# Weight stacks of a convolution made on GpSimd alone and spread over more steps, and a table request moved to the end of a layer

## The chip, the cores and the metric

The kernel runs on one core of a Trainium2 chip. The core has five engines, each with a queue of its own that it works off in order: TensorE (PE, whose weight loads are shown as PEld), VectorE (DVE), ScalarE (ACT), GpSimd (POOL) and SyncE (SP, which here only starts transfers). The metric is the device time of one execution in microseconds; the figure for a kernel is the median of its runs.

## The reference, cut to what matters

A network of four layers, each an attention-like part and a feed-forward part with a residual sum and a layer norm behind each, is applied to `x` of shape (2, 1024, 1024) in float32:

```python
x = _layernorm(x + _L0_attn_ref(x, ...))   # 8 heads of 16, softmax over 1024 keys
x = _layernorm(x + _L0_ffn_ref(x, ...))    # permuted columns, per head up, gelu, down, permuted back
x = _layernorm(x + _L1_attn_ref(x, ...))   # a convolution over 3 positions gives q, k, v; attention in blocks of 128
x = _layernorm(x + _L1_ffn_ref(x, ...))    # product with the signs of the weights, routed scales
x = _layernorm(x + _L2_attn_ref(x, ...))   # selective scan
...                                        # L2_ffn, L3_attn, L3_ffn
```

What the change touches is the preparation of the weights of the convolution in layer 1 and the logarithm and exponential that the layer norms use.

The convolution is

```python
x = lax.conv_general_dilated(inputs, conv_w, window_strides=(1,), padding='SAME', ...) + conv_b
```

with `conv_w` of shape (3, 1024, 768). The kernel computes four neighbouring outputs at a time from six combinations of the inputs, each multiplied with its own combination of the three weight matrices g0, g1, g2. Two of the six are g0 and g2 themselves; the other four are g0 + g1 + g2, g0 - g1 + g2, g0 + 2 g1 + 4 g2 and g0 - 2 g1 + 4 g2 (constant factors are applied to the products later).

## The kernel before, in words

The kernel works through the two batches (b = 0, 1) one after the other, and through all layers for each. All 1024 tokens of a batch stay on chip, as `x` (tokens on the partitions, in eight tiles of 128) and as `xT` (channels on the partitions). `th` names a half of 512 tokens.

The order of the work is written out by hand inside blocks (`with self.tc.manual_schedule()`): within such a block each engine takes its instructions in the order of the program. There is one such block in `l0`, and several in `l1_attn`, one in `l1_ffn`.

**Layer 0 (`l0`).** The block goes through these steps:

- `qkv`: projections to queries, keys and values (L318), eight matmuls for each half, evicted by DVE (L327) or ACT (L325). Queries and keys are spread to their places by eight transfers each on SP's queue (L332); values are transposed on PE (L338) and copied by ACT (L341).
- `maxima(0)`: 16 steps, in each of which PE makes scores (L362) and DVE takes their maxima (L372). The remaining projections (`side`) are laid between these steps.
- `attend(0, turns)`: 16 steps; scores (L397), exponentials on ACT (L405), weighted sums (L415). `turns` adds a step of `maxima(1)` to each.
- `attend(1, e, ...)`: 16 steps of the same for the second half; `e` adds the output projection (L473, L482), the norm of the first four token tiles (statistics L169, L170; `ln_roots`, `ln_scale`, L192), the transposes to `xT` (L136; L103 on DVE, L105 on ACT), the transfers of `xT` to `xd` on SP (`store(tt)` of the layer, L487), and the gathers of permuted rows (`gather(0)`, L497: indirect transfers on GpSimd's queue).
- `blocks(0, e, ...)` and `blocks(1, e)`: per head pair the up product (L515), gelu on ACT (L523), the down product (L533), and an indirect transfer out to `yd` on GpSimd's queue (L546).

**The stacks.** In batch 0 alone, `stacks()` computes the four weight combinations for 24 blocks of 128 x 256 numbers. It is a generator: each `next(made)` does one step. For a block, `load(n)` starts three transfers on SP (L274), `make(n)` does six additions on GpSimd (L280, L282, L284, L285, L286, L288) and three multiplications on ACT (L281, L283, L287), and `store(n)` starts four transfers on SP to `cvd` in DRAM (L292). Three sets of buffers are used in turn: two weight tiles and `third`. Steps are taken from step 6 of `maxima(0)` on, one in every step, through the 16 steps of `attend(0)`. Layer 1's convolution reads `cvd` when it starts.

**The norms' roots.** `ln_roots` calls `rsqrt`: a logarithm (L183) and an exponential (L184) on ACT, then a correction on DVE (L186 to L189). ACT has to hold a table with the function it computes. `table()` asks for the one with both:

```python
def table(self):
    if self.other:
        self.nc.scalar.preload_act_table_set("natural_log_exp_and_others")
    self.other = False
```

`self.other` is set where gelu or silu is used. A load that was asked for shows in the profile as ACT_TABLE_LOAD at L199; one that was put in because a function's table was not there shows at the line of that function (L183, L184, L523, L1284). `l1_attn` calls `table()` at L820, in the middle of its first hand-ordered block, ahead of `root(4)` to `root(7)`, which are the roots of the second half's tiles. No other ACT instruction stands ahead of that call in that block.

The functions as they stand:

Of the kernel before, what the change touches and what calls it, by code (L numbers as in the profile page):

```python
# [8 lines left out]
F = mybir.dt.float32  # L9
# [3 lines left out]
ALU = mybir.AluOpType  # L13
# [4 lines left out]
P = 128  # L18
# [9 lines left out]
class Net:  # L28
# [191 lines left out]
    def l0(self, b):  # L220
        nc, i = self.nc, self.i
# [15 lines left out]
        with self.tc.tile_pool(name=self.nm("l0a"), bufs=1) as lp, self.tc.tile_pool(name=self.nm("l0b"), bufs=2) as tp:  # L237
# [24 lines left out]

            if b == 0:
                self.cvd = self.dp.tile([6, 4, P, D], F, name=self.nm("cvd"))
                third = lp.tile([P, 4, 256], F, name=self.nm("third"))

            def stacks():

                sets = [self.w().rearrange("p (a c) -> p a c", a=4) for _ in range(2)] + [third]
                add = nc.gpsimd.tensor_tensor  # L270

                def load(n):
                    for j in (0, 2, 1):
                        nc.sync.dma_start(  # L274
                            sets[n % 3][:, j, :], i["l1_conv"][n // 4, j][:, n % 4 * 256 : n % 4 * 256 + 256]
                        )

                def make(n):
                    g0, g1, g2, t = [sets[n % 3][:, j, :] for j in range(4)]
                    add(t, g0, g2, ALU.add)  # L280
                    nc.scalar.mul(g2, g2, 4.0)  # L281
                    add(t, t, g1, ALU.add)  # L282
                    nc.scalar.mul(g1, g1, 2.0)  # L283
                    add(g0, g0, g2, ALU.add)  # L284
                    add(g2, t, g1, ALU.subtract)  # L285
                    add(g0, g0, g1, ALU.add)  # L286
                    nc.scalar.mul(g1, g1, 2.0)  # L287
                    add(g1, g0, g1, ALU.subtract)  # L288

                def store(n):  # L290
                    for e, j in enumerate((3, 2, 0, 1)):
                        nc.sync.dma_start(  # L292
                            self.cvd[n // 4, e][:, n % 4 * 256 : n % 4 * 256 + 256], sets[n % 3][:, j, :]
                        )

                load(0)
                load(1)
                yield
                for n in range(24):
                    make(n)  # L300
                    if n:
                        store(n - 1)
                    if n + 2 < 24:
                        load(n + 2)
                    yield
                store(23)
                yield

            nmax = [piece("nmax").rearrange("p (a c) -> p a c", a=4) for _ in range(2)]
            for t in nmax:  # L310
# [274 lines left out]
            def at(extra, n, f):  # L585
                extra.setdefault(n, []).append(f)

            got = {}
            with self.tc.manual_schedule():
                self.table()  # L590
                for s in (1, 0):
                    for _ in qkv(s, 0, False):
                        pass
                for tt in range(4, NT):
                    self.to_xT(tt)
                for tt in range(4, NT):
                    self.add_row(row, tt)
                side = [
                    f for s, th in ((1, 1), (0, 1), (2, 0), (2, 1)) for f in [qkv(s, th, True)]
                    for _ in range(5 if s == 2 else 4)  # L600
                ]
                m0 = maxima(0)
                for n in range(16):
                    next(m0)
                    if b == 0 and n == 6:
                        made = stacks()
                    if b == 0 and n >= 6:
                        next(made)
                    for f in side[: 2 if n < 2 else 1]:
                        next(f)  # L610
                        del side[0]
                for f in side:
                    next(f)
                m = maxima(1)
                turns = {n: [lambda: next(m)] for n in range(16)}
                turns[0].insert(0, lambda: next(m0))
                if b == 0:
                    for n in range(16):
                        turns[n].append(lambda: next(made))
                done0 = attend(0, turns)  # L620
                e = line(0, project, (0, 1, 3, 4, 5, 6, 7, 8, 9))
                e[0].insert(0, lambda: next(m))
                for n in range(4):
                    at(e, 6 + n, lambda n=n: store(n))
                at(e, 9, lambda: gather(0))
                ahead = {n: [lambda tt=tt: turn_o(tt)] for tt, n in enumerate((0, 1, 3, 4))}
                done = attend(1, e, ahead, lambda: done0(1))
                e = line(1, project, (0, 0, 1, 1, 2, 3, 3, 4, 4))
                for n, tt in ((3, 4), (3, 5), (4, 6), (4, 7)):
                    at(e, n, lambda tt=tt: store(tt))  # L630
                for n in (5, 6):
                    at(e, n, lambda: gather(1, 2))
                ahead = {n: [lambda t=t: turn_o(t), lambda t=t: turn_o(t + 1)] for n, t in ((0, 4), (1, 6))}
                blocks(0, e, ahead, lambda: done(1))
                ys = back(0)
                e = line(0, lambda tt: self.add_y(tt, ys), (3, 3, 4, 4, 5, 6, 6, 7, 7))
                for n in (0, 1):
                    at(e, n, lambda: gather(1, 2))
                blocks(1, e)
        return yd[1]  # L640


# [3 lines left out]
    def l1_attn(self, b, yd, op):  # L646
        nc, i = self.nc, self.i
        row = self.row("l1_projb")
        with self.tc.tile_pool(name=self.nm("l1a"), bufs=1) as lp, self.tc.tile_pool(name=self.nm("l1s"), bufs=2) as spool:
# [138 lines left out]
            c = [conv(0, co) for co in range(6)]  # L788
# [8 lines left out]
            with self.tc.manual_schedule():  # L797
                if b == 0:
                    nc.vector.tensor_scalar(cb6, cb, -6.0, None, ALU.mult)
                    nc.vector.tensor_scalar(bq8, bq, 0.125, None, ALU.mult)  # L800
                for co, j in (
                    [(co, j) for j in (1, 2, 3, 0, 4) for co in (0, 1)] + [(2, 1), (2, 2), (2, 3), (0, 5), (1, 5)]
                    + [(2, 4), (2, 0), (2, 5)] + [(co, j) for co in (3, 4, 5) for j in ORDER]
                ):
                    c[co]["load"](j)
                pump()
                ys = [t for q in range(4) for t in (vh[:, q, :HALF], vh[:, q, HALF:])]
                for k, t in enumerate(ys):
                    nc.sync.dma_start(t, yd[k * P : (k + 1) * P, :])
                for k0, k1 in ((0, 2), (2, 4), (4, KD)):  # L810
                    sums(0, one, k0, k1)
                    c[0]["calls"](1, k0, k1)
                product(1, 1)
                product(0, 2)
                product(1, 2)
                sums(0, two)
                product(0, 3)
                product(1, 3)
                sums(0, [c_] + three)
                self.table()  # L820
                self.add_y(4, ys)
                root(4)
                product(0, 0)
                product(1, 0)
                self.add_y(5, ys)
                product(0, 4)
                c[0]["both"]()
                product(1, 4)
                c[1]["both"]()
                self.to_xT(4)  # L830
                sums(0, [e_] + five)
                root(5)
                for j in (1, 2, 3):
                    product(2, j)
                self.add_y(6, ys)
                for co in (0, 1):
                    product(co, 5)
                    c[co]["last"]()
                self.to_xT(5)
                root(6)  # L840
                product(2, 4)
                self.add_y(7, ys)
                product(2, 0)
                c[2]["both"]()
                product(2, 5)
                c[2]["last"]()
                self.to_xT(6)
                root(7)
                later = {
                    (3, 4): [lambda: self.to_xT(7)], (3, 5): [lambda: sums(1, [c_] + one)], (4, 2): [lambda: sums(1, two)],  # L850
                    (4, 4): [lambda: sums(1, [e_])], (5, 2): [lambda: sums(1, three + five)],
                }
                for co in (3, 4, 5):
                    for j in ORDER:
                        product(co, j)
                        if j == 0:
                            c[co]["both"]()
                        for f in later.get((co, j), []):
                            f()
                    c[co]["last"]()  # L860
# [171 lines left out]
            with self.tc.manual_schedule():  # L1032
# [42 lines left out]
                for name in ("l1_ics", "l1_ocs"):  # L1075
                    src, out = self.w(i[name], 32)[:32, :], self.w()[:32, :].bitcast(R)
                    part = self.l1p["l1_part"]
# [1331 lines left out]
```

## Time and profile before

| What | Value |
|---|---|
| Three runs | 4877.68, 4885.57 (median), 4892.11 us |
| The profiled execution | 4882.62 us, of which 4880.8 us are the span of its instructions |
| Mean granted TensorE clock | 0.968 |
| Busy share of the span | PE 92%, DVE 68%, POOL 46%, ACT 44% |
| Stacks (batch 0) | first addition on GpSimd at 66.41 us, last at 194.75 us |
| Table loads on ACT | 59 at L199, 36 at L183, 35 at L184, each 1.283 us |
| Layer 0 of batch 0, first score to first up product (L515) | 31.55 to 252.5 us |
| Layer 0 of batch 1, the same stretch | 2485.0 to 2657.5 us |

All times inside a profile are microseconds from the start of the span, unless marked ns. A row of a timeline gives the start, the duration, the engine, the line of the kernel, the operation, what is written and read, the shape, how often, and in brackets how long the engine stood idle before it and what it had waited for. "L183" is line 183 of the kernel before.

### The profile page before, as it was taken

Reading aid. Unit: us, or ns where it says so; the run is one execution under the profiler, and the core shown is the slowest. Engines: PE = TensorE matmul, PEld = TensorE weight load, DVE = VectorE, ACT = ScalarE, POOL = GpSimd, SP = SyncE. Lnnn points to the kernel's source line nnn. Section 1 sums busy time; section 2 is a strip of 40 time slices with the busy share of each in tenths; the row PEclk is TensorE's granted clock in tenths of the full one; section 3 lists DMA queues with packets and bytes.
Section 4 is the critical chain, followed back from the end, with each engine's and each line's share of the span. In section 5 each row is a group of like instructions: output and inputs, shape, how many; then the busy total and the mean of one; then the engine's idle time right before and its main releaser. Section 6 shows DMA issues by size and latency. Waiting matters only on the chain.

```text
span 4880.8 us, 52994 instructions
## 1 busy us (share of the span) xinstructions
PE 4472.3 (92%) x17736; PEld 2197.7 (45%) x17736; DVE 3334.0 (68%) x4568; ACT 2145.0 (44%) x4273; POOL 2234.3 (46%) x1421
## 2 busy tenths in 40 slices
PE   7999999988888888999999999899888888899999
PEld 3347755433333333565443676553333333335644
DVE  4555266399999998554465643643999999966453
ACT  2542254377665654122015323535776756531310
POOL 5421121088888986040020121212887989840310
PEclk8999999999999999999999999999999989999999
DMA  5355422488888999411121652124888889983100
GB/s 176 114 195 182 126 72 89 131 223 228 231 223 232 253 247 247 170 55 49 52 70 42 231 169 93 63 80 133 219 230 223 222 237 250 250 276 108 62 13 31
DMA packets 315508, 768.09 MB, mean 157 GB/s; under 512 B 40288, under 2 KB 112096, under 8 KB 315236
## 3 DMA queue, kind: packets, MB, share of 16 engines
q1 hardware_dynamic: 307556, 739.52, 53.0%
q0 software_dynamic: 7680, 25.17, 1.5%
q8 instruction: 142, 2.33, 0.2%
q14 instruction: 130, 1.06, 0.1%
HBM read 644.75 MB, written 100.93 MB: 153 GB/s over the span
## 4 chain that ended last, share of the span: by engine, by line
PE 52%; DVE 19%; DMA 9%; issue 5%; POOL 4%; ACT 4%; SPq 1%; DVEq 0%; POOLq 0%; ACTq 0%
PE ps L110 14%; DVE h L1520 9%; PE ps L735 5%; PE ps L1892 5%; PE ps L2202 5%; POOL h L1506 3%; PE ps L1628 3%; DMA h<-dxd 2%; DVE h L1531 2%; DMA xi<-xcd 2%; PE ps L1905 2%; PE ps L1846 2%; PE ps L1542 2%; PE ps L1513 2%; PE ps L1666 2%
## 5 line engine op out<-in xcount | busy, mean ns | idle before, releaser
L1506 POOL TENSOR_TENSOR h<-h,br 128x1024 f32<-128x1024 f32 x512 | 1205.4, 2370 | 104.4 <-DMA h<-dxd 72.9
L1515 ACT ACTIVATE ps<-ps,l_Alog 128x512 f32<-128x512 f32 x1024 | 662.5, 662 | 552.8 <-PE ps L1513 549.8
L1513 PE MATMUL ps<-hl,rep 128*128 128x512 f32 x1024 | 730.3, 717 | 180.8 <-DVE h L1520 148.1
L1520 DVE TENSOR_TENSOR_SCAN h<-ps,hst,h 128x512 f32<-128x512 f32 x512 | 633.5, 1281 | 20.9 <-ACT ps L1515 16.7
L1531 DVE TENSOR_TENSOR h<-h,ps 128x1024 f32<-128x1024 f32 x512 | 616.5, 1204 | 1.3 <-ACT hst L1528 1.3
L1520 DVE TENSOR_TENSOR_SCAN h<-ps,h 128x512 f32<-128x512 f32 x512 | 599.2, 1211 | 19.3 <-ACT ps L1515 19.3
L1628 PE MATMUL ps<-xT,w 128*128 128x512 f32 x1024 | 545.5, 619 | 8.7 <-DVE h L1520 7.5
L1513 PEld LDWEIGHTS ps<-hl,rep 128*128 128x128 f32 x1024 | 200.8, 197 | 610.4 <-DVE h L1520 437.2
L143 POOL TENSOR_TENSOR x<-x,row 128x1024 f32<-128x1024 f32 x80 | 191.0, 2407 | 572.5 <-PE ps L136 532.2
L945 POOL TENSOR_TENSOR s<-s,l1r 128x512 f32<-128x512 f32 x64 | 66.2, 1039 | 555.9 <-DVE l1r L944 507.8
L1542 PE MATMUL ps<-h,sel 128*32 128x512 f32 x2048 | 296.6, 632 | 5.1 <-DVE h L1531 5.1
L1666 PE MATMUL ps<-w,w 128*128 128x512 f32 x512 | 277.7, 626 | 18.6 <-DMA w<-yd 15.7
L1451 POOL TENSOR_TENSOR e<-e,one 128x512 f32<-128x512 f32 x64 | 81.4, 1273 | 450.3 <-ACT xp L1323 317.5
L1628 PEld LDWEIGHTS ps<-xT,w 128*128 128x128 f32 x1024 | 190.2, 195 | 202.8 <-issue 166.3
L1573 PE MATMUL ps<-xT,w 128*128 128x512 f32 x512 | 270.4, 627 | 6.1 <-DVE h L1520 6.1
L1331 DVE SCALAR_TENSOR_TENSOR ps<-xp,l_convw,ps 128x512 f32<-128x512 f32 x192 | 145.1, 756 | 185.9 <-ACT ps L1326 181.3
L158 DVE TENSOR_TENSOR x<-x,ps 128x512 f32<-128x512 f32 x192 | 128.8, 683 | 183.3 <-PE ps L2208 136.2
L1892 PE MATMUL ps<-w,w 128*128 128x512 f32 x512 | 229.7, 596 | 0.0
L110 PE MATMUL ps<-xT,w 128*128 128x512 f32 x512 | 227.8, 597 | 0.0
L2202 PE MATMUL ps<-w,xT 128*128 128x512 f32 x512 | 225.9, 593 | 0.0
L183 ACT ACTIVATE rs<-mv 128x1 f32<-128x1 f32 (+2 forms) x78 | 15.9, 204 | 465.3 <-DVE mv L177 464.8
L372 DVE TENSOR_REDUCE mx<-ps 128x1 f32<-128x512 f32 x256 | 159.0, 683 | 67.9 <-PE ps L362 67.9
(333 smaller groups left out, 7893.1 us busy)
## 6 DMA issues: line engine op xcount, KB each, us to landing
h<-dxd SPq DMA_DIRECT2D x512, 512.0 KB, 8.0
w<-l_in SPq DMA_DIRECT2D x128, 512.0 KB, 6.3
w<-cvd SPq DMA_DIRECT2D x96, 512.0 KB, 4.1
w<-l_out SPq DMA_DIRECT2D x96, 512.0 KB, 8.5
w<-l_conv SPq DMA_DIRECT2D x48, 512.0 KB, 4.4
w<-l_fw SPq DMA_DIRECT2D x32, 512.0 KB, 4.8
xcd<-xo SPq DMA_DIRECT2D x64, 256.0 KB, 6.4
xi<-xcd SPq DMA_DIRECT2D x64, 256.0 KB, 8.7
```

Of the source, the lines that this page charges most:

```text
L110: self.nc.tensor.matmul(out, lhsT, rhs, start=j == 0, stop=j == n - 1)
L1506: nc.gpsimd.tensor_tensor(hs[k], hs[k], norms[of(k)[0]][1].unsqueeze(1).to_broadcast([P, 2, HALF]), ALU.mult)
L1513: nc.tensor.matmul(dA[k, m], rep[:, 4 * m + q, :], hl[u, c][:, jj, :], start=True, stop=True)
L1515: nc.scalar.activation(dA[k, m], dA[k, m], AF.Exp, scale=A[:, g : g + 1])
L1520: nc.vector.tensor_tensor_scan(hs[k][:, m, :], dA.pop((k, m)), hs[k][:, m, :], hst[:, g : g + 1] if u else 0.0, ALU.mult, ALU.add)
L1531: nc.vector.tensor_tensor(hs[k], hs[k], norms[of(k)[0]][3].unsqueeze(1).to_broadcast([P, 2, HALF]), ALU.mult)
L1542: nc.tensor.matmul(py[u, c][32 * j : 32 * j + 32, :], self.sel[:, q, :], hs[k - 1 + j // 2][:, j % 2, :], start=False, stop=q == 3,)
L1573: nc.tensor.matmul(p, w["w"][:, k * P : (k + 1) * P], self.xcols(k, u0, HALF), start=k == 0, stop=k == KD - 1)
L1628: nc.tensor.matmul(p, w["w"][:, k * P : (k + 1) * P], self.xcols(k, u * HALF, HALF), start=k == 0, stop=k == KD - 1)
L1666: nc.tensor.matmul(p, y[:, cc, t * P : (t + 1) * P], wt[:, cc * HALF : (cc + 1) * HALF], start=c2 == 0 and cc == 0, stop=last,)
L1892: nc.tensor.matmul(pa[tt], y[:, cc * HALF + tt * P : cc * HALF + (tt + 1) * P], w[:, cc * HALF : (cc + 1) * HALF], start=c2 == 0 and cc == ...
L2202: nc.tensor.matmul(p, self.xcols(k, tt * P, P), wt[k][:, ns], start=k == 0, stop=False)
```

## The change

In `stacks()` the three multiplications of a block go from ACT to GpSimd. With a fifth buffer for one of the results two of them suffice: the sum and the difference of g0 + g2 and g1 are taken first, then g2 is multiplied by 4 and g1 by 2. There are two sets of buffers in place of three. The order within a step becomes: store of the block before, load of the next block, then the block itself. Steps are taken in two of every three steps of the loops, from step 7 of `maxima(0)` through `attend(0)` and on into `attend(1)`, whose last step with one is 13. The call of `table()` at L820 is removed, and one is put at the end of `l0`'s hand-ordered block, in both batches.

```diff
             if b == 0:
                 self.cvd = self.dp.tile([6, 4, P, D], F, name=self.nm("cvd"))
-                third = lp.tile([P, 4, 256], F, name=self.nm("third"))
+                third = lp.tile([P, 2, 256], F, name=self.nm("third"))
 
             def stacks():
 
-                sets = [self.w().rearrange("p (a c) -> p a c", a=4) for _ in range(2)] + [third]
-                add = nc.gpsimd.tensor_tensor
+                sets = [
+                    [t[:, j, :] for j in range(4)] + [third[:, n, :]]
+                    for n, t in enumerate(self.w().rearrange("p (a c) -> p a c", a=4) for _ in range(2))
+                ]
+                add, times = nc.gpsimd.tensor_tensor, nc.gpsimd.tensor_scalar
+
+                def part(t, n):
+                    return t[:, n % 4 * 256 : n % 4 * 256 + 256]
 
                 def load(n):
                     for j in (0, 2, 1):
-                        nc.sync.dma_start(
-                            sets[n % 3][:, j, :], i["l1_conv"][n // 4, j][:, n % 4 * 256 : n % 4 * 256 + 256]
-                        )
+                        nc.sync.dma_start(sets[n % 2][j], part(i["l1_conv"][n // 4, j], n))
 
                 def make(n):
-                    g0, g1, g2, t = [sets[n % 3][:, j, :] for j in range(4)]
+                    g0, g1, g2, t, o = sets[n % 2]
                     add(t, g0, g2, ALU.add)
-                    nc.scalar.mul(g2, g2, 4.0)
-                    add(t, t, g1, ALU.add)
-                    nc.scalar.mul(g1, g1, 2.0)
+                    add(o, t, g1, ALU.add)
+                    add(t, t, g1, ALU.subtract)
+                    times(g2, g2, 4.0, None, ALU.mult)
                     add(g0, g0, g2, ALU.add)
-                    add(g2, t, g1, ALU.subtract)
-                    add(g0, g0, g1, ALU.add)
-                    nc.scalar.mul(g1, g1, 2.0)
+                    times(g1, g1, 2.0, None, ALU.mult)
+                    add(g2, g0, g1, ALU.add)
                     add(g1, g0, g1, ALU.subtract)
 
                 def store(n):
-                    for e, j in enumerate((3, 2, 0, 1)):
-                        nc.sync.dma_start(
-                            self.cvd[n // 4, e][:, n % 4 * 256 : n % 4 * 256 + 256], sets[n % 3][:, j, :]
-                        )
+                    for e, j in enumerate((4, 3, 2, 1)):
+                        nc.sync.dma_start(part(self.cvd[n // 4, e], n), sets[n % 2][j])
 
                 load(0)
-                load(1)
                 yield
-                for n in range(24):
-                    make(n)
+                for n in range(25):
                     if n:
                         store(n - 1)
-                    if n + 2 < 24:
-                        load(n + 2)
+                    if n < 24:
+                        if n < 23:
+                            load(n + 1)
+                        make(n)
                     yield
-                store(23)
-                yield
...
-                    if b == 0 and n >= 6:
+                    if b == 0 and n >= 6 and n % 3:
                         next(made)
...
                 if b == 0:
                     for n in range(16):
-                        turns[n].append(lambda: next(made))
+                        if n % 3:
+                            turns[n].append(lambda: next(made))
                 done0 = attend(0, turns)
                 e = line(0, project, (0, 1, 3, 4, 5, 6, 7, 8, 9))
                 e[0].insert(0, lambda: next(m))
+                if b == 0:
+                    for n in range(16):
+                        if n % 3 < 2 and n < 14:
+                            at(e, n, lambda: next(made))
...
                 blocks(1, e)
+                self.table()
         return yd[1]
...
                 sums(0, [c_] + three)
-                self.table()
                 self.add_y(4, ys)
```

## The prediction

> **What bounds the kernel now.** I read the page first, then the stage that the change touches against its twin: layer 0 runs twice, and the second time (batch 1) it has no stacks, since they are made once. The page says that TensorE is the bound on average:
>
> ```profile
> PE 4472.3 (92%) x17736; PEld 2197.7 (45%) x17736; DVE 3334.0 (68%) x4568; ACT 2145.0 (44%) x4273; POOL 2234.3 (46%) x1421
> ```
>
> So a stall is worth removing only where PE waits. The table of windows, cut at the same points of the program in both batches (first score matmul L362; first transpose L338; first score of the attention, L397; within half a us of the first transpose ahead of the output projection, L473), shows where batch 0 loses. The columns are window, length, then busy time of PE, PEld, DVE, ACT, POOL, then granted clock, DMA share and GB/s:
>
> ```profile
> 31.55:80.00 48.45, 37.12 (x144) 13.16 (x144) 31.31 (x53) 4.79 (x11) 19.66 (x21) 0.92 0.35 104
> 80.00:106.50 26.50, 17.36 (x60) 6.91 (x60) 11.00 (x21) 8.41 (x21) 22.60 (x33) 0.82 0.58 187
> 106.50:202.00 95.50, 88.86 (x552) 30.10 (x552) 45.40 (x82) 52.24 (x119) 67.48 (x95) 0.84 0.47 148
> ...
> 2485.00:2521.70 36.70, 36.70 (x145) 13.11 (x144) 28.09 (x48) 2.65 (x4) 6.80 (x3) 1.00 0.14 35
> 2521.70:2537.50 15.80, 15.02 (x66) 6.00 (x62) 13.55 (x26) 1.33 (x3) 0.00 (x0) 1.00 0.00 0
> 2537.50:2607.00 69.50, 67.92 (x553) 25.59 (x552) 45.21 (x82) 36.25 (x71) 0.00 (x0) 1.00 0.00 1
> ```
>
> The same PE work takes 170.45 us in batch 0 and 122.00 in batch 1: 48.45 more. About 25 of it is PE standing idle (27.1 against 2.4), the rest PE at a granted clock of 0.82 to 0.92 instead of 1.00, and waits too short to show. The timelines of PE and of ACT say why:
>
> ```profile
> 67.56 1.14 PE L362 MATMUL ps<-kT,qT 32*128 32x512 f32 x8
> 80.96 1.11 PE L338 MATMUL ps<-ident,st 128*128 128x128 f32 x4 [12.26 <-ACT st L325]
> ...
> 105.46 1.11 PE L338 MATMUL ps<-ident,st 128*128 128x128 f32 x4 [8.18 <-ACT st L325]
> ```
>
> ```profile
> 79.92 0.42 ACT L287 ACTIVATE third<-third 128x256 f32<-128x256 f32 x1 [1.75 <-POOL third L286]
> 80.24 0.67 ACT L325 ACTIVATE st<-ps,bqkv 128x512 f32<-128x512 f32 x1
> ```
>
> PE finished the values' matmuls at 67.6, but their eviction L325 stands in ACT's queue behind the stacks' multiplications, and those wait for GpSimd's additions (1.75 us each block). One block a step at 4.9 us on GpSimd is slower than a step of this loop (3.0 us), so ACT, and behind it PE, walks at GpSimd's pace.
>
> The second half of the change is about table loads on ACT:
>
> ```profile
> 325.39 1.28 ACT L199 ACT_TABLE_LOAD   x1
> ...
> 336.03 1.28 ACT L183 ACT_TABLE_LOAD   x1
> ...
> 371.67 0.20 ACT L183 ACTIVATE rs<-mv 128x1 f32<-128x1 f32 x1 [3.66 <-DVE mv L177]
> 371.89 1.28 ACT L184 ACT_TABLE_LOAD   x1
> 373.18 0.20 ACT L184 ACTIVATE rs<-rs 128x1 f32<-128x1 f32 x1
> ```
>
> L199 is the explicit request. After one, logarithm (L183) and exponential (L184) follow with no load between. In layer 1 none runs (no L199 load between 325.39 and 940.43), though line 820 asks for one; so each root loads a table before L183 (36 times) and another before L184 (35 times, and once for L1284). Why the request of line 820 is missing can be read from another row: it is ACT's first instruction in its hand-ordered block, and DVE's first of that block, L799, ran in layer 0:
>
> ```profile
> 28.44 1.66 DVE L799 TENSOR_SCALAR cb<-l_convb 128x6 f32<-128x6 f32 x1
> ```
>
> An instruction without waits at the head of a block floats forward; there the right table was loaded and the request had nothing to do.
>
> **Part 1, the stacks.** Removed: 72 ACT multiplications at 0.42 us. Added on GpSimd: 48 tensor_scalar; additions stay six a block, and each block still issues three loads and four stores on SP. After this nothing on ACT, DVE or PE waits for a stack, and batch 1 is the price without them: 48.45 us less. What GpSimd's pace still touches are two queues. Additions start 0.68 to 0.80 us after one another: six at 0.74 make 4.44. No tensor_scalar of GpSimd is in the trace: from 0.29 (CAST 128x128, half the elements) to 0.80 (the spacing of a two-input addition of this size); the nearest is the one-input AFFINE_SELECT, 0.511 at 128x225, so 0.58 at 256. A block is 4.44 + 2 x 0.58 = 5.6 us (5.0 to 6.0). Two sets in place of three: the next load of g1 waits for the last store (2.3 us to land), then lands (2.3): 4.7 to 5.5 with issues, under 5.6, so GpSimd sets the pace. From the first addition at 66.4, block 21 ends at 66.4 + 22 x 5.6 = 189.6.
>
> GpSimd's queue: gather(0) stands behind block 21. In batch 1 it starts at 2650.47, 165.5 after the first score, so 197.0 here: 7 us spare. Blocks 22 and 23 come behind it, to about 218; the first scatter L546, due at 211.8, is 6 us late, the second (219.6) nearly on time, and o has three buffers. SP's queue: xd store 0 stands behind store(18) and load(20), ready at 172.8 + 3.7 = 176.5, due at 180.1; xd store 3 behind load(22), 187.7 against 193.0. Both are covered; at 6.0 a block xd store 3 is 4 us late, of which 3.7 are slack (gather at 197.0, landing 3.3, PE's L515 at 204.0). The first load keeps its place behind the qT transfers (L332), and the last store, near 221, is long over when layer 1 asks for cvd (306.91 in the trace, so about 259). I take 1.0 us for late scatters and shared DMA (0 to 3).
>
> One new contact: the roots of attend(1) now run at 174.9, beside GpSimd. The rows show what that costs DVE:
>
> ```profile
> 729.94 2.35 POOL L1162 TENSOR_TENSOR lo<-xT,hi 128x512 fp32r<-128x512 f32 x2 [9.16 <-ACT hi L1161]
> 729.96 1.20 DVE L189 TENSOR_TENSOR rs<-rs,rsq 128x1 f32<-128x1 f32 x1
> 731.19 1.65 DVE L192 TENSOR_SCALAR x<-x,mv,rs 128x1024 f32<-128x1024 f32 x1
> ```
>
> L189 takes 0.16 and L192 0.81 without GpSimd; here each waits out the GpSimd instruction. L186, L187, L189 and the first L192 come before PE's transpose: 4 x 0.6 = 2.4, less 0.9 of slack in batch 1, is 1.5 us (0 to 2.0). The Trainium skill, SBUF — State Buffer, Who interferes with whom, says the same against this change: a Vector instruction with two SBUF inputs, or in a 2-port mode, and a GpSimd instruction that reads SBUF exclude one another; the rows agree (1.20 for 0.16). By that rule L436 also waits, which nothing is behind.
>
> Part 1: 48.45 - 1.0 - 1.5 = 45.95 us.
>
> **Part 2, the table.** At layer 0's end the request is the last of its hand-ordered block, behind gelu and L105, so it stays, in both batches. 72 loads go, two come (where the L183 load at 336.03 stood: ACT then idles 21.55 us, which hides the 1.28; without that cover it would cost 1.28 a batch). L183's load runs ahead of its wait and is hidden; L184's 1.283 lies between logarithm and exponential, with DVE waiting (1.78 us idle at L186). It counts only where PE waits behind DVE, so each stretch gives the smaller of its loads on the chain of waits and PE's idle time there:
> - roots 5 and 6 in the convolution: 2.57, PE idle 2.30 (1.31 + 0.99) and 2.27 in batch 1;
> - attention's norms 0 to 2: 3.85 of 6.2 and 7.1;
> - layer 1's second half to 757 us (3167): four loads, 5.13 of 7.4 and 8.9;
> - to its last root: five loads, 6.42, but PE idle only 5.87 and 2.38. Here PE is late next.
>
> Batch 0: 2.30 + 3.85 + 5.13 + 5.87 = 17.15; batch 1: 2.27 + 3.85 + 5.13 + 2.38 = 13.63; 30.8 us. At most all idle time of these stretches, 42.4; at least 0. The Trainium skill, ScalarE: Activation LUTs, What ACT_TABLE_LOAD costs, gives a switch 2.66 us, half of it a drain; here L184 starts 1.29 after its load starts, so the trace does not show the drain. By 2.66 the stretches would be capped by PE's idle time, 42.4 at most.
>
> Sum: 45.95 + 30.8 = 76.75. The profiled execution took 4882.62 (span 4880.8 and 1.8 around it), the median is 4885.57; the difference is the same for both: 4805.9 for a like execution, 4808.8 for the median.
>
> **Rivals.**
> - The request does nothing at its new place either (for: one such request vanished; against: this one has ACT work of its own block in front). Then 4885.57 - 45.95 = 4839.6. Chance 0.08.
> - GpSimd's multiplication is dearer than any row suggests, and gather(0) comes late: from 66.4 + 22d = 200.7, d = 6.1, 0.83 each, every further us of d costs 22. At 1.5 each, d = 7.4: 28.5 late, 4837. Against: one-input rows all lie under 0.6. Chance 0.08.
> - The same mechanism to the other side, GpSimd's queue as the bound of layer 0: slower than before once gather(0) is 76.75 late, d = 9.6, a multiplication of 2.6 us, 3.6 times the addition. At 3.0: d = 10.44, 95.4 late, 4904. Chance 0.04.
> - Forecast as summed, 0.80.
>
> **Numbers.** Best case: 48.45 + 42.4 = 90.9, 4794.7, less 5 for the spread of the three runs (4877.68 to 4892.11). Upper end: the first two rivals, 4840, plus 2. Range 4790 to 4842. 0.3% (14.7 us) is about what can be told from no change: faster 0.94, same 0.02, slower 0.04.
>
> **What would show it.** PE's rows L338 without an ACT wait, clock 1.00 there, 122 to 126 us from the first score to L473; no load at L183, L184 or L1284, one L199 at each layer 0's end; L186 idle near 0.5 in place of 1.78; GpSimd blocks at 5.6 us; gather(0) 165 to 167 us after the first score. A gather later than 169, or PE idle in layer 1 unchanged without the loads, would make it wrong.

## The result and the profile after

The kernel after takes 4812.1 us (median of 4 runs, 4804.34 to 4820.51) against 4884.0 for the kernel before in the same comparison: ratio 0.9852, 95% interval 0.983 to 0.9875. The forecast was 4808.8. The total was met, but two of its terms were not: the first part of the change gave 15 us less than summed, and the second part and the later layers gave more.

The page's line of the engines, profile after:

```profile
PE 4440.4 (92%) x17736; PEld 2192.6 (46%) x17736; DVE 3331.1 (69%) x4568; ACT 2031.3 (42%) x4131; POOL 2278.4 (47%) x1469
```

ACT has 142 instructions less: 72 multiplications and 72 table loads go, two requests come. GpSimd has the 48 multiplications more. The windows of the kernel after (start and end, length, busy PE, PEld, DVE, ACT, POOL, granted clock, DMA share, GB/s), cut at the same instructions as the windows of before in batch 0, except that the third now ends at a score matmul some 4 us into the second attention (202.03 in the profile before, 158.98 here); after it come the stretches to the first up-projection (L514, the reader of gather(0)), to layer 1's first q tile and to layer 2:

```profile
32.70:73.80 41.10, 41.06 (x144) 15.51 (x145) 27.80 (x47) 2.06 (x3) 8.88 (x7) 0.88 0.23 68
73.80:89.50 15.70, 14.92 (x64) 5.98 (x60) 13.54 (x26) 1.33 (x3) 14.56 (x20) 1.00 0.41 129
89.50:158.95 69.45, 67.88 (x553) 25.57 (x552) 45.51 (x82) 36.15 (x71) 64.18 (x87) 1.00 0.45 143
158.95:220.85 61.90, 50.28 (x300) 17.28 (x292) 23.67 (x43) 32.62 (x66) 55.16 (x71) 0.94 0.55 174
220.85:308.10 87.25, 83.34 (x376) 34.18 (x377) 47.87 (x93) 46.15 (x82) 40.62 (x48) 0.96 0.52 174
308.10:889.25 581.15, 559.51 (x2958) 371.74 (x2958) 316.74 (x594) 166.66 (x519) 93.72 (x68) 0.99 0.41 134
```

The granted clock is a share of full speed; the clock records of these traces hold only 1.0 and 0.5, and a stretch at 0.5 is called half clock below. The last three stretches in the kernel before:

```profile
202.00:252.50 50.50, 50.12 (x300) 17.74 (x292) 20.66 (x42) 32.56 (x66) 5.33 (x6) 1.00 0.22 64
252.50:337.70 85.20, 80.63 (x377) 33.12 (x377) 48.58 (x94) 46.08 (x82) 27.11 (x31) 1.00 0.48 162
337.70:937.20 599.50, 565.89 (x2958) 373.75 (x2958) 317.03 (x594) 211.22 (x554) 92.23 (x67) 0.97 0.40 130
```

Read as differences, before minus after: from the first score to the cut in the second attention 170.45 - 126.25 = 44.2 us gained; to the first up-projection 11.4 lost; to layer 1 another 2.05 lost, at a clock of 0.96 in place of 1.00; layer 1 of batch 0 gains 18.35, layer 1 of batch 1 (594.75 to 578.35) 16.4. The first score comes 1.15 us later, the other stretches together gain 5.05. The sum is 69.4, the difference of the two spans (4880.8 and 4811.4).

The timelines of PE, of GpSimd and of SP in the kernel after show the loss:

```profile
73.80 0.66 PE L337 MATMUL ps<-ident,st 128*128 128x128 f32 x4
...
220.90 3.79 PE L514 MATMUL ps<-t,w 64*128 64x512 f32 x8 [9.66 <-DMA t<-xd,idx]
```

```profile
71.13 0.73 POOL L284 TENSOR_TENSOR w<-w 128x256 f32<-128x256 f32 x1 [31.98 <-PE ps L361]
...
75.21 0.85 POOL L289 TENSOR_SCALAR w<-w 128x256 f32<-128x256 f32 x1
...
77.63 0.73 POOL L284 TENSOR_TENSOR w<-w 128x256 f32<-128x256 f32 x1
...
214.38 0.72 POOL L291 TENSOR_TENSOR w<-w 128x256 f32<-128x256 f32 x1
216.92 1.18 POOL L496 DMA_INDIRECT t<-xd,idx  x1 [1.82 <-DMA xd<-xT]
```

```profile
212.68 0.38 SPq L486 DMA_DIRECT2D xd<-xT  x1
```

PE's wait for ACT at the values' transposes (12.26 us before) is gone. A block takes 77.63 - 71.13 = 6.5 us, the multiplication 0.85 and the addition 0.73. Block 21 ends at 215.1, the gather starts at 216.92, and PE stands idle for 9.66 us before its reader. In batch 1 of the kernel before, the gather starts 4.0 us after the last transposed copy ends; here that copy ends at 200.19, so by this measure the gather is 12.7 us late. For its last 1.82 us it waits for the store of the fourth normalised tile, which SP issues only at 212.68: the store stands in SP's queue behind the stacks' transfers, and those go at GpSimd's pace.

The second part, at a root of layer 1: timelines of ACT and of DVE in the kernel after, then DVE's row at the same root in the kernel before:

```profile
306.53 1.28 ACT L199 ACT_TABLE_LOAD   x1
...
758.67 0.20 ACT L183 ACTIVATE rs<-mv 128x1 f32<-128x1 f32 x1 [7.67 <-DVE mv L177]
758.91 0.20 ACT L184 ACTIVATE rs<-rs 128x1 f32<-128x1 f32 x1
```

```profile
759.14 0.16 DVE L186 TENSOR_TENSOR rsq<-rs 128x1 f32<-128x1 f32 x1 [0.50 <-ACT rs L184]
```

```profile
802.79 0.16 DVE L186 TENSOR_TENSOR rsq<-rs 128x1 f32<-128x1 f32 x1 [1.78 <-ACT rs L184]
```

The request stays, runs in ACT's idle time, and all 72 loads are gone. DVE waits 0.50 us for the exponential in place of 1.78.

### The profile page after: what moved, and what is told of

Read it like the earlier page. It is cut to its first block, busy times and chain, and to the rows that moved or that the text cites. A ratio compares the mean times of both kernels' runs of the same rounds, so it can differ in the third digit from the quotient of the medians.

```text
span 4811.4 us, 52825 instructions
## 1 busy us (share of the span) xinstructions
PE 4440.4 (92%) x17736; PEld 2192.6 (46%) x17736; DVE 3331.1 (69%) x4568; ACT 2031.3 (42%) x4131; POOL 2278.4 (47%) x1469
## 3 DMA queue, kind: packets, MB, share of 16 engines
q14 instruction: 129, 1.06, 0.1%
## 4 chain that ended last, share of the span: by engine, by line
PE 52%; DVE 17%; DMA 10%; issue 5%; POOL 5%; ACT 4%; SPq 1%; POOLq 0%; DVEq 0%; ACTq 0%
PE ps L110 15%; DVE h L1524 9%; PE ps L740 5%; PE ps L2206 5%; PE ps L1896 5%; POOL h L1510 3%; DMA h<-dxd 3%; PE ps L1632 2%; PE ps L1909 2%; PE ps L1850 2%; DVE h L1535 2%; DMA xi<-xcd 2%; PE ps L1546 2%; PE ps L136 1%; PE ps L1517 1%
## 5 line engine op out<-in xcount | busy, mean ns | idle before, releaser
L1632 PEld LDWEIGHTS ps<-xT,w 128*128 128x128 f32 x1024 | 188.7, 193 | 200.8 <-issue 163.9
L183 ACT ACTIVATE rs<-mv 128x1 f32<-128x1 f32 (+2 forms) x78 | 15.9, 203 | 502.6 <-DVE mv L177 502.2
```

Of the source, the lines that this page charges most:

```text
L1632: nc.tensor.matmul(p, w["w"][:, k * P : (k + 1) * P], self.xcols(k, u * HALF, HALF), start=k == 0, stop=k == KD - 1)
```

## Experiments

Times below are medians, each against the kernel before on the same chip (4892.3 for the first four, 4890.2 for the next four, 4883.1 for the last two). The expectations count from the first score, and "the second attention's first score" in them is the cut described above. "The whole change" in the first eight is its first comparison, 71.9 us less than before.

**The first part alone.** The request goes back to its old place:

```
-                self.table()          # end of layer 0
...
+                self.table()          # before add_y(4) in layer 1
```

> The change's first part alone: stacks on GpSimd, the table request back at its old place in layer 1. Theory (the late gather ate part of the gain): from the first score to PE's first up-projection matmul (the reader of gather(0)) some 188 us as with the whole change, against 221.0 before; GpSimd's block 6.47 us; gather(0) 17 to 20 us later than the 165.5 of batch 1; 72 table loads at L183, L184 and the one behind A_log's exponential, as before; 27 to 33 us less than before, 4851 to 4857. Rival (the forecast's own term is right and the profiled run was a poor one): gather(0) within 167 us of the first score and 46 us less, 4838.

Measured: 4855.5, 36.9 us less (ratio 0.9925, 0.9905 to 0.9945). The windows, cut as above:

```profile
32.45:160.65 128.20, 125.81 (x755) 47.24 (x756) 87.26 (x155) 39.54 (x77) 90.02 (x114) 0.95 0.37 117
160.65:221.15 60.50, 50.13 (x300) 17.46 (x292) 22.53 (x43) 32.63 (x66) 54.06 (x69) 0.97 0.55 173
221.15:307.85 86.70, 81.93 (x376) 33.49 (x376) 47.63 (x93) 46.28 (x82) 40.50 (x48) 0.98 0.53 176
307.85:908.60 600.75, 566.05 (x2958) 373.48 (x2958) 317.42 (x594) 211.44 (x554) 93.49 (x68) 0.97 0.39 130
```

Layer 0 repeats the whole change: gather(0) 184.8 us after the first score, up-projection at 188.7, 275.4 us from the first score to layer 1 as in the kernel after (306.15 before). Layer 1 is that of before (600.75 against 599.50). So the late gather belongs to this part and was no chance of one run. The median lies between theory (27 to 33) and rival (46); its interval holds both, and the stages decide for the theory.

**The second part alone.** The kernel before with the request at layer 0's end:

```
                 blocks(1, e)
+                self.table()
         return yd[1]
```

> The change's second part alone: the kernel before with the request at layer 0's end. Theory (each stall that goes takes its half-clock time after it along): 35 to 39 us less than before, 4845 to 4849, of it some 25 in PE's idle time of layer 1 and 8 to 12 in PE's busy time at half clock there. Rival (the forecast's term: idle time alone): 30.8 less, 4853, with PE's busy time in layer 1 unchanged. Second rival (the two parts need one another): under 25 less.

Measured: 4857.9, 34.5 us less (0.9929, 0.9913 to 0.9946). Its layer 1 in batch 0 and in batch 1:

```profile
344.80:924.95 580.15, 559.94 (x2958) 370.84 (x2958) 316.30 (x594) 166.42 (x519) 93.04 (x68) 0.98 0.41 135
2748.35:3325.50 577.15, 557.83 (x2958) 370.25 (x2958) 299.90 (x570) 166.54 (x519) 92.51 (x68) 0.99 0.36 121
```

599.50 - 580.15 = 19.35 and 594.75 - 577.15 = 17.6, together 36.95. The same matmuls (x2958) keep PE busy 565.89 - 559.94 = 5.95 us less, 4.4 in batch 1: 10.4 us are clock, 26.6 idle time. The theory's split holds, and the idle time alone does not make the gain; the median lies just under the 35 to 39 expected. The two parts together (36.9 + 34.5 = 71.4) are the whole change (71.9): neither needs the other.

**Two blocks behind the gather.**

```
-                        if n % 3 < 2 and n < 14:
+                        if n in (0, 1, 3, 4, 6, 10, 12, 13):
                             at(e, n, lambda: next(made))
...
+                if b == 0:
+                    for n in (1, 2):      # first MLP loop
+                        at(e, n, lambda: next(made))
```

> The whole change, but stack blocks 20 and 21 are made behind gather(0), two of the last steps inside the first MLP loop; nothing else differs. Theory (GpSimd's queue makes gather(0) late): gather(0) starts two blocks (12.9 us) earlier, 2 to 6 us late instead of 18.7; PE's idle time before its reader falls from 9.7 to under 3, with no half clock after it; 8 to 12 us less than the whole change. Rival (the transposed activations' stores or their landing are late, not the queue): the gather starts no more than 4 us earlier and the time is within 3 us. Second rival: blocks 20 to 23 behind the gather delay the scatters by 13 us or more and the gain goes there: PE idle at the readers of yd instead, no gain.

Measured: 4820.1, 72.3 us less (0.985, 0.9832 to 0.9868): no gain over the whole change. Windows to the up-projection and on to layer 1, and PE's longest wait in the second:

```profile
159.50:212.75 53.25, 51.34 (x300) 17.82 (x292) 22.42 (x42) 32.63 (x66) 42.77 (x55) 0.97 0.56 174
212.75:311.00 98.25, 84.15 (x377) 34.45 (x377) 50.05 (x94) 46.22 (x82) 51.84 (x62) 0.95 0.51 167
```

```profile
267.94 5.12 PE L514 MATMUL ps<-t,w 64*128 64x512 f32 x16 [6.65 <-DMA t<-xd,idx]
```

The gather starts at 206.14, 0.3 us later than the copies allow, and its stretch gets 8.65 us shorter: the queue is what made it late. The next stretch gets 11.0 us longer. The first scatter waits behind blocks 20 to 22 until 235.73, though its tile is written at 225.4; the roots of the second half meet the last block on GpSimd, and the second half's gathers come so late that PE waits 6.65 us for them. The second rival is right in kind, with the wait at these gathers and not at the readers of yd. Another 3.50 us PE waits at L426 for a copy of DVE (at 218.29); the profile gives no reason, and two later runs that leave blocks 20 and 21 ahead of the gather wait 2.84 and 3.15 us at the same place, so this wait need not come from the edit.

**The stacks two steps earlier.**

```
-                    if b == 0 and n == 6:
+                    if b == 0 and n == 4:
                         made = stacks()
-                    if b == 0 and n >= 6 and n % 3:
+                    if b == 0 and n >= 4 and n % 3:
...
-                        if n % 3 < 2 and n < 14:
+                        if n in (0, 1, 3, 4, 6, 10, 12, 13):
```

> The whole change, but the stacks begin two steps of the maxima earlier (step 4 in place of 6), so that their first load stands ahead of the last qT transfers in SP's queue; 22 blocks stand ahead of gather(0) as before. Theory (GpSimd's queue alone makes the gather late): first addition at 52 to 58 us in place of 71.1, block 21 done by 200, gather(0) within 3 us of 165.5 after the first score, PE's idle time of 9.7 before its reader gone; 11 to 14 us less than the whole change, 4798 to 4802. Rival (a block slows when it runs beside the maxima's DVE work, or qT's transfers are now late): first addition early but block 21 no earlier than 208, or PE waits for qT in the second maxima; under 5 us less.

Measured: 4807.0, 85.4 us less (0.9824, 0.9808 to 0.9841).

```profile
158.90:212.70 53.80, 51.66 (x300) 17.80 (x292) 22.87 (x42) 32.63 (x66) 44.20 (x57) 0.97 0.54 166
```

First addition at 56.20, GpSimd free at 202.8, the gather at 208.36 (177.2 after the first score, not the 165.5 expected): its last 5.5 us it waits for the activations' stores. The stretch falls from 61.9 to 53.8, 8.1 us of the 11.4 lost, and PE's wait ahead of the reader is gone, as the theory has it. The gather is late by a second, smaller limit: the stores on SP stand behind the stacks' transfers. PE does not feel it. What is left of the stretch is at the roots of the norm, which run beside GpSimd:

```profile
184.33 1.06 PE L136 MATMUL ps<-ident,x 128*128 128x128 f32 x8 [0.61 <-DVE x L192]
...
187.56 1.51 PE L396 MATMUL ps<-qT,kT 32*128 32x512 f32 x6 [1.12 <-DVE xT L103]
189.00 1.94 PE L414 MATMUL ps<-pt,v 128*32 128x512 f32 x8
```

PE waits 0.61 + 1.12 us there, and its busy time in the stretch is 1.5 us above that of the kernel before (51.66 against 50.12): the matmuls behind these waits ran at half clock (L414, 1.94 us in place of 1.06). Together that is the 3.3 us to the 50.50 of the kernel before.

**At the first step.** The load of block 0 goes to step 0, of the blocks three come after the gather's step as before:

```
+                    if b == 0 and n == 0:
                         made = stacks()
+                    if b == 0 and (n == 0 or n % 3 == 1 or n > 4 and n % 3):
...
+                        if n in (0, 1, 3, 10, 12, 13):
```

> The whole change, but the stacks begin at the first step of the maxima (their first two loads stand ahead of the second half's kT transfers in SP's queue); 22 blocks stand ahead of gather(0) as before. Theory (what is still late two steps earlier, 177.2 us after the first score for gather(0), comes from GpSimd's backlog, which also holds the activations' stores on SP): first addition at 43 to 47 us in place of 56.2, block 21 done at 190 to 193, gather(0) 165 to 168 us after the first score, PE's stretch from the second attention's first score to the first up-projection at 50.5 to 51 in place of 53.8; 2 to 5 us less than with the start at step 4, so 87 to 91 less than before. Rival (transfers of kT or qT, which the maxima need, now stand behind stack transfers on SP): PE idle over 2 us in the maxima or a later second maxima, no gain over the start at step 4.

Measured: 4815.8, 74.4 us less (0.9842, 0.9818 to 0.9866). SP's waits from 38 to 62 us:

```profile
SPq L280 <- PE ps L317: 17.4, 2, 10.6
```

The two sets lie in weight buffers that PE's projections (L317) read until then: the loads wait 17.4 us for them, at the head of SP's queue, with kT's transfers behind (59.92, against 48.21 with the start at step 4), and PE waits 1.1 us for kT. The first addition comes at 49.37, the second block's at 61.09. GpSimd is free at 203.7, as with the start at step 4 (202.8), and the gather still waits 4.98 us for the stores. There is no gain over the start at step 4, as the rival has it, but PE's 1.1 us is under the rival's 2: the earlier start in the program bought nothing because the buffers were not free.

**The activations' stores from ACT's queue.**

```
-                nc.sync.dma_start(
+                (nc.sync if tt >= 4 or b else nc.scalar).dma_start(
                     xd[tt // 4]...
```

> The start at step 4, and the four stores of the normalised activations in layer 0's first half of batch 0 are issued from ACT's queue in place of SP's. Theory (there gather(0) waits 5.5 us for those stores, which stand in SP's queue behind the stacks' stores and loads): gather(0) starts when GpSimd is free, 170 to 173 us after the first score in place of 177.2, with a DMA wait under 1 us; 1 to 4 us less than with the start at step 4, so 86 to 89 less than before. Rival (the transposes, not SP's queue, make the stores late): gather(0) still waits 4 us or more for them, no gain.

Measured: 4825.9, 64.3 us less (0.9867, 0.9845 to 0.989), worse than both expected. Little was to be had: with the start at step 4 PE did not wait for the gather any more. ACT's timeline:

```profile
183.30 0.59 ACT L105 COPY xT<-ps 128x512 f32<-128x512 f32 x1 [1.77 <-PE ps L136]
200.82 0.39 ACTq L486 DMA_DIRECT2D xd<-xT  x1
201.26 2.06 ACT L404 ACTIVATE pt<-ps 128x512 f32<-128x512 f32 x4 [17.37 <-DMA w<-l_conv]
```

The first store is issued 17 us after its copy, when a load of a stack lands, and the attention's exponentials stand behind it on ACT: PE waits 14.85 us for them, and the gather starts at 221.85. So here, too, a store was held by a stack's load, by the releaser that the profile infers; on SP only the gather stood behind the store, on ACT the exponentials did. Why an xd store has to wait for a load of l_conv the profile does not say, and it stays open.

**The request one norm later in layer 1**, behind ACT's first instructions there (both flags set so that nothing else asks for the table):

```
                 blocks(1, e)
-                self.table()
+                self.other = False
...
                 self.to_xT(4)
+                self.other = True
+                self.table()
```

> The whole change, but the request stands in layer 1 behind the first transposed copies (one norm later than the old place, and no longer ACT's first instruction of its block). Theory (a request at the head of a block is moved forward, one behind an ACT instruction stays): one L199 load in each layer 1, two loads left at L183 and two at L184 (the first root of each batch), a time within 6 us of the whole change, 65 to 80 less than before. Rival (requests in layer 1 vanish wherever they stand): no L199 load there, 36 and 35 loads at L183 and L184, 33 to 40 less than before.

Measured, one run: 4824.7, 65.5 us less. ACT's timeline and its groups of loads:

```profile
326.39 1.28 ACT L184 ACT_TABLE_LOAD   x1
...
333.41 0.60 ACT L105 COPY xT<-ps 128x512 f32<-128x512 f32 x1
334.03 1.28 ACT L199 ACT_TABLE_LOAD   x1
```

```profile
L183 ACT ACT_TABLE_LOAD x2 | 2.6, 1283 | 0.0
L184 ACT ACT_TABLE_LOAD x2 | 2.6, 1283 | 0.0
```

The request stays as soon as it is not ACT's first of its block: four loads are left of 72. That bears out the forecast's reading that the old one moved to the front of its block and vanished; the move itself stands in no trace and is inferred from the place alone. The time, a single run, is 6.4 us from the whole change, just beyond the expected 6; the whole change's own runs lie further apart (4804.3 to 4820.5).

**Without the multiplications.**

```
-                    times(g2, g2, 4.0, None, ALU.mult)
...
-                    times(g1, g1, 2.0, None, ALU.mult)
```

> The whole change without the two multiplications on GpSimd (left out, so the stacks are not the reference's). Theory (the multiplication's 0.85 us in place of the forecast's 0.58, and the first addition's 71 in place of 66, make the gather late): block of 4.6 to 4.9 us in place of 6.47, block 21 done at 172 to 180, gather(0) 165 to 168 us after the first score, PE's idle time of 9.7 before its reader gone; 12 to 15 us less than the whole change, so 84 to 87 less than before. Rival (something else in the new order holds the gather): gather(0) later than 175 after the first score, under 6 us less.

Measured: 4812.3, 77.8 us less (0.984, 0.9819 to 0.9862).

```profile
160.10:210.65 50.55, 50.13 (x300) 17.75 (x292) 20.88 (x43) 32.62 (x66) 16.54 (x22) 1.00 0.40 120
```

The stretch to the up-projection is that of the kernel before (50.50): all 11.4 us are back. But block 21 ends at 198.0, not 172 to 180. A block takes 4.6 us of GpSimd (70.90 to 75.48), and 21 of them are done at 168.65. Then GpSimd stands idle; its row at the last block ahead of the gather, and SP's longest wait between 150 and 200 us:

```profile
193.41 0.73 POOL L284 TENSOR_TENSOR w<-w 128x256 f32<-128x256 f32 x1 [24.76 <-DMA w<-l_conv]
```

```profile
SPq L484 <- DVE xT L103: 28.4, 2, 25.2
```

The load of that block stands in SP's queue behind the store of the first normalised tile (L484 here), and SP waits 25.2 us for that tile. So the last block ahead of the gather waits for PE's transposes, and the gather, 173.2 us after the first score, starts 1.4 us later than the copies allow, which PE does not feel. GpSimd is also idle when the roots run, so their contact is gone as well (L189 takes 0.16 us). The run therefore gives back the late gather and the contact together and does not part the two. Layer 0 up to layer 1 gains 8.1 us over the whole change (267.3 against 275.4). In the median the run is 5.9 us below the whole change, short of the theory's 12 to 15 and just within the rival's 6, and the gather lies between the two; that PE no longer waits for the gather is shown in the stage, not in the total.

**The whole change and the early start once more, side by side.**

> The whole change again, unaltered, as the measure for the early start beside it. 70 to 75 less than before. Its profile, by the theory of the late gather: gather(0) starts 11 to 14 us later than 4.0 us after the last transposed copy (12.7 in the first profile); by the rival (that profile was a chance) under 6. PE's first wait for qT is 3.3 to 4.7 us as in every profile since, not the 2.5 of the kernel before, with half clock behind it.

> The start two steps earlier again, unaltered, beside the whole change on the same chip. Theory: gather(0) 1 to 4 us later than 4.0 us after the last transposed copy in place of 12.7, PE's stretch from the second attention's first score to the first up-projection 53 to 54 in place of 61 to 62, and the later stages alike, so 7 to 14 us less than the whole change. Rival (the gain of the first pair of runs was the spread of the later layers): within 4 us of it.

Measured: 4813.7, 69.5 us less (0.9862, 0.9846 to 0.9879), and 4808.8, 74.4 us less (0.9854, 0.9837 to 0.987). Windows to the up-projection, first of the whole change, then of the early start:

```profile
156.75:218.40 61.65, 50.27 (x300) 17.26 (x292) 24.01 (x43) 32.63 (x66) 55.47 (x71) 0.97 0.56 174
```

```profile
156.10:210.95 54.85, 52.49 (x300) 17.91 (x292) 23.17 (x42) 32.61 (x66) 45.32 (x57) 0.94 0.56 170
```

The gather is 12.2 us late in the first and 0.6 in the second, and layer 1 begins at 306.15 and 294.85: 11.3 us in the profiles, as the theory has it, with spans of 4809.5 and 4798.9. The medians differ by 4.9 with overlapping intervals, under the expected 7 to 14. What a stage of layer 0 gains is seen in every profile; 5 to 10 us in the total are lost in the spread of the rest: layers 2 and 3 of batch 0 take 1530.4 us in the profile before and 1531.8 to 1541.0 in the eleven others. In the early start the 4.35 us that its stretch is longer than the 50.50 of before stem from the roots again: PE waits 0.64 + 1.12 us there, and the mean granted clock is 0.59 from 185.0 to 192.4. PE's first wait for qT is 2.54 and 2.35 us here, so the 3.3 to 4.7 of the earlier profiles (2.96 in the start at the first step) was spread too. The early start is the best version that was run, and its lead over the change as made is shown in the stage, not in the total.

## Why the prediction came out as it did

**What stood.** The mechanism of the first part: no L337 waits for a stack, and from the values' transposes to the second attention PE takes what batch 1 takes (15.70 + 69.45 us against 15.80 + 69.50). The contact at the roots costs 0.48 + 1.12 = 1.6 us of PE's idle time behind L192 and the transposed copies (1.5 was taken); that no half clock followed was the better case, since behind the same contact the early start ran at half clock and lost 3.3 and 4.35 us in its two profiles. The mechanism of the second part: one L199 at each layer 0's end, no load left at L183, L184 or A_log's exponential, a wait at L186 of 0.50.

**The term that failed: the block on GpSimd.** The step priced the multiplication at 0.58 us from a one-input row of another operation (0.511 at 128x225), and bounded it by the addition (0.73 busy, 0.80 spacing). It takes 0.85, with 0.93 from start to start, dearer than the two-input addition and outside the bound; the block is 6.47 in place of 5.6 (5.0 to 6.0), and 0.7 of these 0.87 us are the two multiplications. The first addition came at 71.1 in place of 66.4: its load stands behind the qT transfers, which wait for an eviction on ACT, and that ran at 60.89 in place of 55.73 in this profile with its slow start. By the prediction's own count, 66.4 + 22d against 200.7, that makes (6.47 - 6.1) x 22 + 4.7 = 12.8 us late. Block 21 ended at 215.1, 14.4 us past 200.7, since the block beside Vector's norm took 7.9 us; the up-projection came 15.7 us later than batch 1 has it (188.2 us after the first score against 172.5), 9.66 of them in PE's wait for the gather and 6.0 ahead of it. The 12.7 us of the gather above count from the last transposed copy and hold the slack, so that they come out beside 12.8 is chance. So the second rival's mechanism happened, with 0.85 us in place of its 1.5 and 15.7 in place of its 28.5. Its argument against ("one-input rows all lie under 0.6") compared other operations, at half the size or with 225 elements. The Trainium skill, GPSIMD Engine Reference, Engine selection, says that on GpSimd two-input operations are about twice slower than on Vector and one-input ones run at roughly line rate; here the one-input operation was the slower of the two on GpSimd, 0.85 against 0.73, and the measurement decides.

**Part 1 in numbers.** 45.95 were forecast. In the profiled pair layer 0, from the first score to layer 1, gives 306.15 - 275.4 = 30.75, 15.2 less. Three stretches are longer than summed: 4.25 us from the first score to the second attention (126.25 against batch 1's 122.0); 11.4 to the up-projection, of which 9.66 are the wait for the gather and 1.6 the contact; 2.05 behind it, where PE starts at half clock. Of these 17.7 the forecast had held back 2.5, 1.5 for the contact and 1.0 for late scatters. The 4.25 are in part a chance of the start: after PE's first wait for qT, 4.67 us, it ran 10.24 us at half clock, which the profile before did not show after its 2.48. Where the prediction said what would make it wrong, it named a gather later than 169 us after the first score; it came at 184.2.

**Part 2 in numbers.** 30.8 were forecast, 18.35 + 16.4 = 34.75 came, 36.95 alone. The step capped each stretch by PE's idle time. Idle time fell by 25.0, 5.8 less than forecast; but PE's busy time for the same matmuls fell by 9.7, a term that the step put at nothing. The last root shows it, PE before and after:

```profile
807.65 1.03 PE L136 MATMUL ps<-ident,x 128*128 128x128 f32 x8
813.64 1.97 PE L136 MATMUL ps<-ident,x 128*128 128x128 f32 x8 [4.96 <-DVE x L192]
815.40 9.03 PE L110 MATMUL ps<-xT,w 128*128 128x512 f32 x16
```

```profile
766.95 1.03 PE L136 MATMUL ps<-ident,x 128*128 128x128 f32 x8
768.56 1.09 PE L136 MATMUL ps<-ident,x 128*128 128x128 f32 x8 [0.57 <-DVE x L192]
769.49 7.04 PE L110 MATMUL ps<-xT,w 128*128 128x512 f32 x16
```

The idle time falls by 4.39 us, and the two groups behind it by another 0.88 + 1.99: after the long stall they ran at half clock. By the clock records, layer 1 of batch 0 has 30.7 us at half clock before and 17.1 after. The Trainium skill, TensorE: Matmul & The Clock Gate, The HAM clock gate, puts it so: after an idle window of about 3.4 us the clock is halved, and the window runs freely, so its place against the stall is chance. The trace agrees in the length: the half-clock stretches of the two profiles are 3.41, 6.83, 10.24 or 13.65 us, but for the first of each (5.07 and 5.68). As a threshold for a stall the figure does not hold here: in the profile before a stall of 2.50 us (to 665.43) was followed by half clock, one of 3.15 (to 735.58) was not.

**Why the total held all the same.** Of the profiled pair's 69.4 us, 7.4 less than the 76.75 summed: 15.2 short in part 1 and 1.15 at the first score, 3.95 more in part 2 and about 5 more in the remaining stretches, which hold no step of the sum (layers 2 and 3 of batch 1 alone 4.35). The medians stand 4.0 further apart than the two profiled executions, which brings 73.5 against 4885.57. That the total came within 3.3 us of the forecast is luck: part 1 short, part 2 beyond its term and the spread of the rest nearly cancelled.

## What to carry to other kernels

An operation that the trace does not have is bounded by the same engine's rows in both directions beyond them, not between them; where its count times the error (22 blocks here) eats the slack of a queue, that slack is the number to compute. A stall on the tensor engine cost its idle time and often some microseconds at half clock behind it (26.6 and 10.4 us in layer 1, with the second part alone), so a wait taken away, or a new one, is priced with both. Work moved from an engine that others wait for (ACT) onto an idle one (GpSimd) still has to leave that engine's queue, and the DMA queue that serves it, before the next thing that others wait for; starting sooner moved the wait to the DMA queue, moving work behind the gather moved it to the scatters.

## What was not expected of the hardware

GpSimd's multiplication of a tile by a constant (128x256, f32) takes 0.85 us, its addition of two such tiles 0.73. Beside Vector's scaling of the norm (L192) the same multiplication stretches to 1.52 and 1.28 us (at 183.62 and 186.23 in the profile after). Waits of PE as short as 0.64 and 1.12 us, close together, were followed by a granted clock of 0.59 over 7.4 us (the early start's second profile). A store issued from ACT's queue held that queue for 17.4 us, by the inferred releaser until a load that SP had issued landed; the cause stays open.
